# Re-ordering the first part of a Strassen gated-FFN kernel: scalings, normalisations and copies on ScalarE, the order of two token tiles, and the mask counts

## The chip, the cores and the metric

One core of one Trainium2 chip. The metric is device time of one execution in microseconds (us): median of three runs 524.1 (524.1, 522.62, 524.27). Engines are named as in the profile: PE is TensorE's matrix product, PEld its weight load, DVE VectorE, ACT ScalarE, POOL GpSimd, SP the engine that issues the DMAs. Each engine works through its instructions in order; an instruction that waits holds up all that stand behind it on its engine.

## What is computed

```python
def reference(data, weight, mask, ln_w, gate_w, up_w, down_w):
    x = data                                    # 2 x 1024 x 512, float32
    xn = _layernorm(x)                          # over the last axis
    block_mask = mask.reshape(nb, 32, kb, 32).astype(float32).sum(axis=(1, 3)) > 0
    w_masked = weight * (block_mask, each entry repeated over its 32 x 32 block)
    s = einsum('bsk,nk->bsn', xn, w_masked)     # 512 x 512 weight
    nx = xn * rsqrt(mean(xn^2) + 1e-5) * ln_w
    g = einsum('bsh,ih->bsi', nx, gate_w)       # 1792 x 512
    u = einsum('bsh,ih->bsi', nx, up_w)         # 1792 x 512
    f = einsum('bsi,hi->bsh', silu(g) * u, down_w)   # 512 x 1792
    return x + s * silu(f)
```

## The kernel before

**Tiling.** The 2048 tokens are four token tiles t = 0 to 3 of 512, each of four sub-tiles i of 128 rows; the 512 features are four chunks c of 128. A sub-tile is loaded (`load_x`, L119), its mean and variance are taken on DVE (`stats`, L125), a tile's scale and offset are made in three steps (`factors`, L130: DVE, a square root on ACT, DVE) and applied (`normalise`, L144, on ACT or DVE). PE turns it over chunk by chunk into a bank (`transpose`, L153), from which a copy (`evacuate`, L159, on ACT) or a subtraction (`outer_b`, L195, on DVE) reads it. `rms_factor` (L169) takes the RMS factor from the same variances: four small DVE operations and a square root on ACT.

**The products.** All products are made by a two-level Strassen scheme: seven outer products q, each of seven inner products m of 128x128 by 128x512. Weights come in seven groups g = 0 to 6 of gate and up rows, and the masked 512x512 weight as group 7. One pair (g, q) is an *instance* j (`instance`, L328): seven products into banks x (m = 1, 6, 7, 4), y (m = 5, 3) and z (m = 2). There are three banks X, two Y, one Z and two V; V holds transposes, gates and the small results. Within an instance: z is seeded with a copy of x on ACT before product 2 adds to it (L345); y and x are saved in the middle (a *snapshot*, L350 to L355, on ACT where there are no earlier sums to add, else an add on DVE); and the final values (*totals*, L357 to L365) are DVE adds, or an ACT copy where there is nothing to add. "x_2" below is bank x of instance 2.

Instances 0 to 15 are q = 1 and 2 of each group. They read only token tiles 0 and 1. Instances 16 to 55 are q = 6, 5, 7, 3, 4 of each group and need tiles 2 and 3 as well. After them, seven sets of 25 products with the down weights.

**Operands.** Token differences are made by `outer_b` (L195) and `inner_b` (L212), on DVE or POOL; weights are loaded (`load_a`, L255), scaled by ln_w in two halves (`scale_a`, L260, on ACT; group 7 is masked instead, `mask_a`, L284, on POOL), and summed on POOL: `inner_a` for q = 1, 2 (L307: four adds of 128x2x128), `outer_a` (L289: four adds of 128x512) for the other q, whose results are stored to DRAM (`store_w`, L300), loaded back later (`load_w`, L303) and summed by `inner_a` again (four adds of 128x5x128). The running sums of a group's first two instances are likewise stored (L454) and loaded back (L455, tensor `acc_dram`). The mask is loaded (`load_mask`, L270), summed along rows on DVE (`mask_rows`, L276), and summed over blocks by a product into a V bank, `pm` (`mask_blocks`, L279), after which DVE writes which blocks are kept.

**What sets the order.** The order is written by hand. `at(pos, fn)` (L69) puts a step at a position; at the end all steps are sorted by position (equal ones in the order in which they were put in) and emitted, and each engine's queue is that order restricted to its own instructions. Position 7*j + offset belongs to instance j: products stand at offsets 0, 2, 3, 4, 6, 8, 12 (m = 1, 5, 2, 6, 3, 7, 4), the snapshot or total one position after its product. One position is about 0.86 us, and `T(us) = (us - 14.9) / 0.86` (L641) turns a time into a position. Nothing but this order and the data decides when a step runs: what stands behind a waiting step on the same engine waits too.

The steps of the first part are in L664 to L751: statistics and normalisation of the tiles, transposes, evacuations, token differences (L682 to L718), scalings and weight sums per group (L721 to L742, with `p` the position of a group's instance q = 1, `rest` that of its q = 6), and the mask (L745 to L749).

Of the kernel before, what the change touches and what calls it, by code (L numbers as in the profile page):

```python
# [31 lines left out]
def tile_masked_linear_gated_ffn(  # L32
# [36 lines left out]
    def at(pos, fn, *args):  # L69
        events.append((pos, len(events), fn, args))  # L70
# [13 lines left out]
    def slot(tag, name=None):  # L84
        i, n = ring[tag]
        ring[tag][0] += 1
        return mem[:, first_slot[tag] + i % n, :]

    def slots(i, n):
        return mem[:, i : i + n, :]  # L90
# [3 lines left out]
    def bank(tag, name):  # L94
        return ps.tile([P, W], F32, tag=tag, name=name, bufs=PSB[tag])

    def add(eng, o, a, b, op=ALU.add):
        eng.tensor_tensor(o, a, b, op)  # L98

    dve, pool, act = nc.vector, nc.gpsimd, nc.scalar  # L100
# [68 lines left out]
    def rms_factor():  # L169

        def first():
            nc.vector.tensor_scalar_add(rms, agg[:, :, :, 1], EPS)
            nc.vector.reciprocal(rms, rms)
            nc.vector.tensor_mul(rms, agg[:, :, :, 1], rms)
            nc.vector.tensor_scalar_add(rms, rms, EPS)
        return [first, lambda: nc.scalar.activation(rms, rms, AF.Sqrt)]
# [72 lines left out]
    def w_slots(g):  # L249

        if g == 0:
            return F["q"], F["a1"] + 4
        return (F["s"], F["s"] + 5) if g % 2 else (F["q"], F["a1"] + 4)
# [53 lines left out]
    def inner_a(g, part, k0=0, n=2):  # L307

        if part == 1:
            i, si, qs = F["a1"] + 2 * (g % 3), F["s"] + 2 * (g % 2), (1, 2)  # L310
        else:
            i, si, qs = *w_slots(g), BLOCKS
        a, s = slots(i + k0, n), slots(si + k0, n)
        a11, a21, a12, a22 = (a[:, :, k * P : (k + 1) * P] for k in range(4))
        s1, s2, s3, s4 = (s[:, :, k * P : (k + 1) * P] for k in range(4))
        for k in range(n):
            aop[g, qs[k0 + k]] = {1: a11[:, k], 2: a12[:, k], 3: s4[:, k], 4: a22[:, k],
                                  5: s1[:, k], 6: s2[:, k], 7: s3[:, k]}
        return [lambda: add(pool, s1, a21, a22), lambda: add(pool, s2, s1, a11, ALU.subtract),
                lambda: add(pool, s4, a12, s2, ALU.subtract), lambda: add(pool, s3, a11, a21, ALU.subtract)]  # L320

    def weights(g, q, m):
        if q < 3 and m in (1, 2, 4):
            return aq[g, 0, q - 1][:, {1: 0, 2: 2, 4: 3}[m] * P :][:, :P]
        return aop[g, q][m]


    def instance(j, g, q, prior, dest, after):  # L328


        st = {}

        seeded = j > 0

        def mm(m, tag, key, first):
            if first and key not in st:
                st[key] = bank(tag, f"{key}_{j}")
            nc.tensor.matmul(st[key], weights(g, q, m), operand(q, m), start=first and not (key == "z" and seeded),  # L338
                             stop=True, skip_group_check=True)

        def seed():

            if seeded:
                st["z"] = bank("Z", f"z_{j}")
                nc.scalar.copy(st["z"], st["x"])  # L345
            else:
                st["s1"] = slot("s2", f"s1_{j}")
                nc.scalar.copy(st["s1"], st["x"])

        def snap(key, name, i):  # L350
            s = st[name] = slot(name, f"{name}_{j}")
            if prior is None:
                nc.scalar.copy(s, st[key])  # L353
            else:
                add(dve, s, st[key], prior(i))  # L355

        def total(key, name, i):  # L357
            if key == "z" and not seeded:
                name = "s1"
            if name:  # L360
                add(dve, dest(i), st[key], st[name])
            elif prior is None:
                nc.scalar.copy(dest(i), st[key])  # L363
            else:
                add(dve, dest(i), st[key], prior(i))  # L365

        at(EARLY.get((j, 0), 7 * j + 1), seed)
        for off, m, tag, first, snapshot, out in (
            (0, 1, "X", True, None, None),
            (2, 5, "Y", True, ("s5", 3), None),  # L370
            (3, 2, "Z", True, None, (None, 0)),
            (4, 6, "X", False, ("s2", 1), None),
            (6, 3, "Y", False, None, ("s2", 1)),
            (8, 7, "X", False, None, ("s5", 3)),
            (12, 4, "X", False, None, (None, 2)),
        ):
            key, pos = tag.lower(), 7 * j + off
            at(EARLY.get((j, m), pos), mm, m, tag, key, first)
            if snapshot:
                at(pos + 1, snap, key, *snapshot)  # L380
            elif out:
                at(pos + 1, total, key, *out)
                after(out[1], pos + 1)


    def group(g, where):
# [254 lines left out]
    T = lambda us: (us - 14.9) / 0.86  # L641
# [14 lines left out]
    def plan(pos, step, todo):  # L656
        for i, fn in enumerate(todo):
            at(pos + step * i, fn)
# [4 lines left out]
            nc.tensor.matmul(b[:, :P], ident, ident, start=True, stop=True, skip_group_check=True)  # L663

    at(T(1.4), lambda: warm(30, bank("V", "idle")))
    for t, p, step in ((0, T(8.2), 0), (1, T(13.4), 0), (2, 15.0, 1.3), (3, 22.0, 1.3)):
        plan(p, step, factors(t))
    for i in range(TT):
        half = act if i < 2 else dve
# [8 lines left out]
    at(T(8.2), scale_a, 0, 0, 1, pool)  # L678
    for c in range(KC):
        at(T((10.7, 11.3, 11.9, 14.0)[c]), evacuate, 0, c, act)  # L680
        at(T((17.4, 16.0, 18.9, 18.3)[c]), evacuate, 1, c, act)
    for us, q, m in ((15.9, 1, 5), (16.6, 1, 6), (17.2, 1, 7), (17.8, 2, 5), (18.4, 1, 4), (19.0, 2, 6),  # L682
                     (19.6, 2, 7), (20.3, 2, 4)):
        at(T(us), inner_b, q, m, dve)
# [2 lines left out]
            for n in (0, 1):  # L687
                at(8, outer_b, q, k, n, None)
    at(T(16.4), scale_a, 1, 0, 0)
    for i, (R, K, g) in enumerate(((0, 1, 1), (1, 0, 0), (1, 1, 0))):  # L690
        at(T(19.2 + 2 * i), scale_a, g, R, K)
    for i in range(TT):
        at(9.6 + 1.3 * i, stats, 2, i)
        at(17.2 + 1.3 * i, stats, 3, i)
        at(17.7 + 1.2 * i, normalise, 2, i, act)
        at(27.0 + 1.9 * i, normalise, 3, i, dve)
    plan(24.8, 1.3, rms_factor())

    for t, p0 in ((2, 31.0), (3, 45.0)):
        n = t % 2  # L700
        for k, c in enumerate((2, 3, 0, 1)):
            for i in range(TT):
                at(p0 + 2 * k + 0.01 * i, transpose, t, c, i, "V")
            if c >= 2:
                at(p0 + 2 * k + 1.2, evacuate, t, c, act)
            else:
                at(p0 + 2 * k + 1.2, outer_b, 5, c, n, dve)
                at(p0 + 2 * k + 1.21, outer_b, 7, c, n, dve)
    for k in (0, 1):
        for n in (0, 1):  # L710
            at(52, outer_b, 3, k, n, None)
    for n, p0 in ((0, 40), (1, 54)):
        for k in (0, 1):
            at(p0 + 1.5 * k, outer_b, 6, k, n, dve)
            at(p0 + 2.2 + 1.7 * k + (16 if n == 0 else 4), outer_b, 4, k, n, pool)
    for q, p in ((6, 57), (5, 66), (7, 76), (4, 89), (3, 113)):
        for off, m, eng in ((0, 5, dve), (3, 6, dve), (5.5, 7, pool), (7.5, 4, pool)):
            at(p + off, inner_b, q, m, eng)  # L718


    for g in range(G + 1):  # L721
        p, rest = 7 * where[g, 1], 7 * where[g, BLOCKS[0]]
        prepare = scale_a if g < G else lambda g, R, K: mask_a(R, K)
        for K in range(2):
            if g > 2:
                at(p - 22, load_a, g, 0, K)
            if g > 1:
                at(p - 14 + 1.5 * K, prepare, g, 0, K)
                at(p - 10, load_a, g, 1, K)
            if g > 0:  # L730
                at(p - 4 + 1.5 * K, prepare, g, 1, K)
        if g:
            plan(p - 8, 1, inner_a(g, 1))
        else:
            plan(T(7.4), 0, inner_a(0, 1, 0, 1))
            plan(T(10.0), 0, inner_a(0, 1, 1, 1))
        sums = {0: 10, G: p + 15}.get(g, p + 1)
        for i, q in enumerate((7, 5, 6, 3)):
            at(sums + 1.6 * i, outer_a, g, q, pool)
        at(sums + 7.5, store_w, g)  # L740
        at(rest - 29 if g else rest - 11, load_w, g)
        plan(rest - 13 if g else rest - 9, 2.5, inner_a(g, 2, 0, 5))  # L742
# [1 line left out]
        for off, fn in zip((8, 30, 32, 34, 36, 37), outer_d(f)):  # L744
            at(7 * where[f, BLOCKS[0]] + off, fn)  # L745
    for i, (R, K) in enumerate(QUADS):
        at(56, load_mask, R, K)
        at(63 + 2 * i, mask_rows, R, K)
    at(71, mask_blocks)  # L749
    at(120, rms_store)  # L750
    for t in range(NTT):  # L751
        at(END + 13, rms_rows, t)
# [17 lines left out]
    for o, q in enumerate(DOWN):  # L770
# [9 lines left out]
        for k, m in enumerate((5, 6, 7, 4)):  # L780
            pos = END + (-26, -17, -8, -5)[k] if o == 0 else D(o - 1)((3, 8, 12, 18)[k])
# [6 lines left out]
        for k in range(4):  # L788
            pos = END + (-22, -18, -11, -9)[k] if o == 0 else D(o - 1)(10) + 2.5 * k
# [84 lines left out]
```

## Time and profile before

| | |
|---|---|
| median of three runs | 524.1 us |
| profiled execution, its own time | 524.07 us |
| its span in the trace | 522.2 us (1.9 less) |
| granted TensorE clock | 1.00 |
| first product of instance 16 (first that needs tiles 2 and 3) | near 121.7 us |
| POOL busy | 378.2 us (72%) |
| ACT busy | 154.6 us (30%) |
| DMA queue 1 | 60000 packets, 137.53 MB, 73.8% of 16 engines' span |

Of the page's 40 slices (13 us each) these rows show the first part on the left:

```profile
PE   8889999999999999999999999999999999999996
DVE  5897798767696877959687896989645654457736
ACT  3868656431332232233233222321100101001111
POOL 5496689978896978969678896977544564739960
PEclk9999999999999999999999999999999999999999
DMA  9559798889829486575996867499897599476372
```

Each digit is the busy share of a slice in tenths, 9 being 90% or more. A line of a timeline reads: start, length, engine, line of the kernel, operation, output<-input, shape, number of instructions taken together, and in brackets the engine's idle time before it with what ended it. A line of a list of groups reads: line, engine, operation, shape, count | busy us, mean ns of one | idle before, with its main releaser. A line of the list of waits reads: engine, tile, line, what it waited for: us in all, times, the longest.

### The profile page before, as it was taken

How to read it: one execution, taken by the hardware profiler on the slowest of the kernel's cores; microseconds unless marked ns; L12 is line 12 of the kernel's file. 1: busy time of each engine (PE TensorE's matmuls, PEld its weight loads, DVE VectorE, ACT ScalarE, POOL GpSimd, SP SyncE). 2: the span in 40 equal slices, each digit the busy share in tenths (PEclk: the TensorE clock that was granted, in tenths of full speed). 3: DMA queues.
4: the chain of work that ended last, by engine and by line, in shares of the span. 5: the costliest groups of instructions: out<-in, count | busy, mean ns of one | idle time of the engine just before them, and what ended most of it. 6: DMA issues, size and time to landing. Idle time of an engine off the chain costs nothing.

```text
span 522.2 us, 4847 instructions
## 1 busy us (share of the span) xinstructions
PE 509.0 (97%) x1269; PEld 230.7 (44%) x1269; DVE 383.7 (73%) x557; ACT 154.6 (30%) x286; POOL 378.2 (72%) x301
## 2 busy tenths in 40 slices
PE   8889999999999999999999999999999999999996
PEld 8333443444444444444444444443444444444443
DVE  5897798767696877959687896989645654457736
ACT  3868656431332232233233222321100101001111
POOL 5496689978896978969678896977544564739960
PEclk9999999999999999999999999999999999999999
DMA  9559798889829486575996867499897599476372
GB/s 312 210 213 347 294 331 331 317 301 325 321 110 313 161 282 238 210 244 185 381 364 231 293 221 270 154 341 387 295 386 267 187 355 347 157 251 204 148 232 80
DMA packets 60314, 138.35 MB, mean 265 GB/s; under 512 B 5744, under 2 KB 13184, under 8 KB 56192
## 3 DMA queue, kind: packets, MB, share of 16 engines
q1 hardware_dynamic: 60000, 137.53, 73.8%
q10 hardware_dynamic: 288, 0.52, 0.3%
q8 instruction: 10, 0.16, 0.1%
q14 instruction: 16, 0.13, 0.1%
HBM read 81.40 MB, written 56.63 MB: 264 GB/s over the span
## 4 chain that ended last, share of the span: by engine, by line
PE 75%; DVE 9%; issue 2%; ACT 0%; DVEq 0%
PE x L338 26%; PE dx L557 14%; PE y L338 14%; PE dy L557 8%; DVE mem L98 7%; PE z L338 6%; PE dz L557 5%; DVE mem L402 2%; PE dv L557 1%; PE half L568 1%; DVE mask_sums L277 0%; DVE mem L547 0%; PE pm L281 0%; ACT silu L540 0%; DVEq L402 0%
## 5 line engine op out<-in xcount | busy, mean ns | idle before, releaser
L98 POOL TENSOR_TENSOR mem<-mem 128x512 f32<-128x512 f32 (+4 forms) x266 | 344.4, 1314 | 107.7 <-ACT mem L363 20.3
L338 PE MATMUL x<-mem 128*128 128x512 f32 x448 | 214.6, 595 | 4.0 <-ACT mem L353 2.4
L338 PEld LDWEIGHTS x<-mem 128*128 128x128 f32 x448 | 83.4, 190 | 109.2 <-issue 92.6
L98 DVE TENSOR_TENSOR mem<-x,mem 128x512 f32<-128x512 f32 x136 | 92.4, 685 | 45.6 <-PE x L338 44.3
L338 PE MATMUL y<-mem 128*128 128x512 f32 x224 | 114.8, 594 | 0.9 <-ACT mem L353 0.5
L98 DVE TENSOR_TENSOR mem<-mem 128x512 f32<-128x512 f32 (+2 forms) x93 | 106.9, 1151 | 7.6 <-PE dx L557 4.4
L557 PE MATMUL dx<-mem 128*128 128x512 f32 x174 | 78.3, 592 | 0.0
L98 DVE TENSOR_TENSOR mem<-y,mem 128x512 f32<-128x512 f32 x96 | 65.8, 685 | 15.5 <-PE y L338 12.8
L345 ACT COPY z<-x 128x512 f32<-128x512 f32 x55 | 31.4, 571 | 125.0 <-PE x L338 125.0
L338 PEld LDWEIGHTS y<-mem 128*128 128x128 f32 x224 | 41.8, 190 | 53.9 <-issue 47.3
L338 PE MATMUL z<-mem 128*128 128x512 f32 x112 | 57.4, 594 | 0.7 <-ACT z L345 0.7
L557 PEld LDWEIGHTS dx<-mem 128*128 128x128 f32 x174 | 33.1, 190 | 41.6 <-issue 40.7
L557 PE MATMUL dy<-mem 128*128 128x512 f32 x98 | 44.5, 592 | 0.0
L402 DVE TENSOR_TENSOR mem<-gate,mem 128x512 f32<-128x512 f32 x56 | 37.4, 681 | 1.7 <-ACT gate L397 1.2
L397 ACT ACTIVATE gate<-mem 128x512 f32<-128x512 f32 x56 | 33.1, 602 | 19.0 <-DVE mem L402 10.0
L530 POOL TENSOR_TENSOR mem<-mem 128x512 f32<-128x512 f32 x16 | 24.9, 1563 | 17.6 <-DMA mem<-s_dram 17.2
L338 PEld LDWEIGHTS z<-mem 128*128 128x128 f32 x112 | 20.9, 190 | 26.2 <-issue 22.3
L98 DVE TENSOR_TENSOR mem<-z,mem 128x512 f32<-128x512 f32 x41 | 28.0, 684 | 3.2 <-PE z L338 3.2
L557 PEld LDWEIGHTS dy<-mem 128*128 128x128 f32 x98 | 18.6, 190 | 23.4 <-issue 23.2
L540 ACT ACTIVATE silu<-mem 128x512 f32<-128x512 f32 x15 | 9.0, 602 | 64.6 <-DVE mem L98 48.3
L98 DVE TENSOR_TENSOR mem<-dx,mem 128x512 f32<-128x512 f32 x16 | 11.1, 691 | 20.1 <-PE dx L557 20.1
L557 PE MATMUL dz<-mem 128*128 128x512 f32 x56 | 25.2, 592 | 0.0
(61 smaller groups left out, 227.3 us busy)
## 6 DMA issues: line engine op xcount, KB each, us to landing
h_dram<-mem SPq DMA_DIRECT2D x98, 256.0 KB, 2.6
mem<-h_dram SPq DMA_DIRECT2D x28, 768.0 KB, 6.8
w_dram<-mem SPq DMA_DIRECT2D x8, 1280.0 KB, 6.2
mem<-w_dram SPq DMA_DIRECT2D x8, 1280.0 KB, 6.9
acc_dram<-mem SPq DMA_DIRECT2D x8, 1024.0 KB, 5.5
mem<-acc_dram SPq DMA_DIRECT2D x8, 1024.0 KB, 4.9
mem<-in_gu SPq DMA_DIRECT2D x28, 256.0 KB, 4.4
s_dram<-mem SPq DMA_DIRECT2D x16, 256.0 KB, 5.1
```

The costliest lines, as they stand in the source:

```text
L98: eng.tensor_tensor(o, a, b, op)
L338: nc.tensor.matmul(st[key], weights(g, q, m), operand(q, m), start=first and not (key == "z" and seeded), stop=True, skip_group_check=True)
L345: nc.scalar.copy(st["z"], st["x"])
L397: nc.scalar.activation(gate[key], t(), AF.Silu)
L402: nc.vector.tensor_mul(a(), gate[key], b())
L530: at_later.append(lambda: nc.gpsimd.tensor_tensor(s_tile, s_tile, rms_bc[t], ALU.mult))
L540: nc.scalar.activation(b[0][:, part], y[:, part] if source is None else source(), AF.Silu)
L557: nc.tensor.matmul(st[key], w(), b(), start=first and key != "z", stop=True, skip_group_check=True)
L568: nc.tensor.matmul(st[half.start][:, half], w(), b()[:, half], start=False, stop=True, skip_group_check=True)
```

## The change

Only positions change (and in one place the choice between two tiles' order); the instructions and DMAs are the same in kind and number.

- `total` on ACT (instances q = 1 and q = 5 that have nothing to add): the copy of z goes from one position behind its product to 2.3 behind it, which is after the snapshot of x.
- Tile 2: factors from position 15.0 to 14.5, statistics in steps of 1.2 instead of 1.3, normalisation on ACT at 30.2, 37.0, 40.9 and 44.0 instead of 17.7, 18.9, 20.1 and 21.3. Tile 3: normalisation on DVE at 26.5 + 2.4i instead of 27.0 + 1.9i. RMS factor from 24.8 to 22.2.
- Tile 1's evacuations of chunks 0, 2 and 3 from positions 2.9, 4.7 and 4.0 to 5.6, 6.0 and 3.14.
- Three early scalings (second half of group 1's first weights, group 0's second rows) from 5.0, 7.3 and 9.7 to 5.2, 8.7 and 9.8. In the queue of ACT their order against the evacuations and snapshots changes with that.
- Tile 3 is transposed at 37.5 and tile 2 at 51.5, where tile 2 stood at 31 and tile 3 at 45; the token differences that need them stand some six positions later, and for the two tiles in the other order.
- Per group: the scalings of the q = 1, 2 weights from p - 14 and p - 12.5 to p - 10.4 and p - 7.3; those of the other rows from p - 4 and p - 2.5 to p - 3.1 and p - 1.9 (group 2: p - 4.3 and p - 3.1); the inner weight sums start at p - 7 instead of p - 8.
- Mask: loads from 56 to 62, row sums from 63 in steps of 2 to 68 in steps of 1.5, block sums from 71 to 76.

```diff
--- before.py
+++ after.py
@@ -379,8 +379,10 @@
             if snapshot:
                 at(pos + 1, snap, key, *snapshot)
             elif out:
-                at(pos + 1, total, key, *out)
-                after(out[1], pos + 1)
+
+                pos += 2.3 if prior is None and m == 2 and seeded else 1
+                at(pos, total, key, *out)
+                after(out[1], pos)
 
 
     def group(g, where):
@@ -663,7 +665,7 @@
             nc.tensor.matmul(b[:, :P], ident, ident, start=True, stop=True, skip_group_check=True)
 
     at(T(1.4), lambda: warm(30, bank("V", "idle")))
-    for t, p, step in ((0, T(8.2), 0), (1, T(13.4), 0), (2, 15.0, 1.3), (3, 22.0, 1.3)):
+    for t, p, step in ((0, T(8.2), 0), (1, T(13.4), 0), (2, 14.5, 1.3), (3, 22.0, 1.3)):
         plan(p, step, factors(t))
     for i in range(TT):
         half = act if i < 2 else dve
@@ -678,7 +680,7 @@
     at(T(8.2), scale_a, 0, 0, 1, pool)
     for c in range(KC):
         at(T((10.7, 11.3, 11.9, 14.0)[c]), evacuate, 0, c, act)
-        at(T((17.4, 16.0, 18.9, 18.3)[c]), evacuate, 1, c, act)
+        at((5.6, T(16.0), 6.0, 3.14)[c], evacuate, 1, c, act)
     for us, q, m in ((15.9, 1, 5), (16.6, 1, 6), (17.2, 1, 7), (17.8, 2, 5), (18.4, 1, 4), (19.0, 2, 6),
                      (19.6, 2, 7), (20.3, 2, 4)):
         at(T(us), inner_b, q, m, dve)
@@ -687,16 +689,16 @@
             for n in (0, 1):
                 at(8, outer_b, q, k, n, None)
     at(T(16.4), scale_a, 1, 0, 0)
-    for i, (R, K, g) in enumerate(((0, 1, 1), (1, 0, 0), (1, 1, 0))):
-        at(T(19.2 + 2 * i), scale_a, g, R, K)
+    for pos, (R, K, g) in zip((5.2, 8.7, 9.8), ((0, 1, 1), (1, 0, 0), (1, 1, 0))):
+        at(pos, scale_a, g, R, K)
     for i in range(TT):
-        at(9.6 + 1.3 * i, stats, 2, i)
+        at(9.6 + 1.2 * i, stats, 2, i)
         at(17.2 + 1.3 * i, stats, 3, i)
-        at(17.7 + 1.2 * i, normalise, 2, i, act)
-        at(27.0 + 1.9 * i, normalise, 3, i, dve)
-    plan(24.8, 1.3, rms_factor())
-
-    for t, p0 in ((2, 31.0), (3, 45.0)):
+        at((30.2, 37.0, 40.9, 44.0)[i], normalise, 2, i, act)
+        at(26.5 + 2.4 * i, normalise, 3, i, dve)
+    plan(22.2, 1.3, rms_factor())
+
+    for t, p0 in ((3, 37.5), (2, 51.5)):
         n = t % 2
         for k, c in enumerate((2, 3, 0, 1)):
             for i in range(TT):
@@ -708,12 +710,12 @@
                 at(p0 + 2 * k + 1.21, outer_b, 7, c, n, dve)
     for k in (0, 1):
         for n in (0, 1):
-            at(52, outer_b, 3, k, n, None)
-    for n, p0 in ((0, 40), (1, 54)):
+            at(58, outer_b, 3, k, n, None)
+    for n, p0 in ((1, 46), (0, 60)):
         for k in (0, 1):
             at(p0 + 1.5 * k, outer_b, 6, k, n, dve)
-            at(p0 + 2.2 + 1.7 * k + (16 if n == 0 else 4), outer_b, 4, k, n, pool)
-    for q, p in ((6, 57), (5, 66), (7, 76), (4, 89), (3, 113)):
+            at(p0 + 2.2 + 1.7 * k + (16 if n == 1 else 4), outer_b, 4, k, n, pool)
+    for q, p in ((6, 63), (5, 70), (7, 78), (4, 90), (3, 113)):
         for off, m, eng in ((0, 5, dve), (3, 6, dve), (5.5, 7, pool), (7.5, 4, pool)):
             at(p + off, inner_b, q, m, eng)
 
@@ -725,12 +727,12 @@
             if g > 2:
                 at(p - 22, load_a, g, 0, K)
             if g > 1:
-                at(p - 14 + 1.5 * K, prepare, g, 0, K)
+                at(p - (10.4, 7.3)[K], prepare, g, 0, K)
                 at(p - 10, load_a, g, 1, K)
             if g > 0:
-                at(p - 4 + 1.5 * K, prepare, g, 1, K)
+                at(p - ((3.1, 1.9) if g != 2 else (4.3, 3.1))[K], prepare, g, 1, K)
         if g:
-            plan(p - 8, 1, inner_a(g, 1))
+            plan(p - 7, 1, inner_a(g, 1))
         else:
             plan(T(7.4), 0, inner_a(0, 1, 0, 1))
             plan(T(10.0), 0, inner_a(0, 1, 1, 1))
@@ -744,9 +746,9 @@
         for off, fn in zip((8, 30, 32, 34, 36, 37), outer_d(f)):
             at(7 * where[f, BLOCKS[0]] + off, fn)
     for i, (R, K) in enumerate(QUADS):
-        at(56, load_mask, R, K)
-        at(63 + 2 * i, mask_rows, R, K)
-    at(71, mask_blocks)
+        at(62, load_mask, R, K)
+        at(68 + 1.5 * i, mask_rows, R, K)
+    at(76, mask_blocks)
     at(120, rms_store)
     for t in range(NTT):
         at(END + 13, rms_rows, t)
```

## The prediction

> **What bounds the kernel now.** I read the page's first lines (busy time) and the kind of work in the chain that ended last, then the list of what PE waited for, then PE's timeline for where those waits are, and last the other engines' timelines around them.
>
> ```profile
> PE 509.0 (97%) x1269; PEld 230.7 (44%) x1269; DVE 383.7 (73%) x557; ACT 154.6 (30%) x286; POOL 378.2 (72%) x301
> PE 75%; DVE 9%; issue 2%; ACT 0%; DVEq 0%
> ```
> ```profile
> PE x L338 <- ACT mem L353: 2.4, 2, 1.3
> PE x L338 <- DVE mem L98: 1.5, 7, 0.2
> PE pm L281 <- DVE mask_sums L277: 1.2, 1, 1.2
> PE z L338 <- ACT z L345: 0.7, 1, 0.7
> ```
> ```profile
> 22.44 1.12 PE L338 MATMUL x<-mem 128*128 128x512 f32 x2 [1.13 <-ACT mem L353]
> 36.03 1.10 PE L338 MATMUL x<-mem 128*128 128x512 f32 x2 [1.31 <-ACT mem L353]
> 45.52 1.12 PE L338 MATMUL z<-mem 128*128 128x512 f32 x2 [0.66 <-ACT z L345]
> 85.77 0.41 PE L281 MATMUL pm<-mask_sums,blockones 128*128 128x64 f32 x2 [1.16 <-DVE mask_sums L277]
> ```
>
> PE is busy 509.0 of 522.2 us, and the granted clock is 1.00 throughout. Products start 0.858 us apart (74.70 to 76.42 is two). Adding up how far the starts fall behind that pitch from 17.5 us to 86 us gives 7.7 us. No reordering of this part can save more than that, and all the edits touch this part. The bulk of it: y_0 and x_0 waiting for ACT's snapshots (0.67 and 1.40; x_0 is bank x of instance 0), x_2's snapshot at 36.03 (1.47), transposes and z_4 at 44.5 to 48 (0.57, 0.88, 0.38), the mask counts (1.33).
>
> **Instances 0 and 1: the snapshots.** ACT's timeline of before:
>
> ```profile
> 19.06 0.59 ACT L164 COPY mem<-pt 128x512 f32<-128x512 f32 x1 [0.55 <-DVE mem L98]
> 19.54 0.59 ACT L353 COPY mem<-y 128x512 f32<-128x512 f32 x1
> 20.02 1.09 ACT L164 COPY mem<-pt 128x512 f32<-128x512 f32 x2
> 20.97 0.94 ACT L266 ACTIVATE mem<-mem,lnw_sb 128x256 f32<-128x256 f32 x2
> 21.78 0.60 ACT L353 COPY mem<-x 128x512 f32<-128x512 f32 x1
> ```
>
> The snapshot of y_0 stands behind an evacuation that waits 0.55 for DVE, and that of x_0 behind two more evacuations (1.09) and a scaling (0.94). In the new order y_0's snapshot comes directly after the scaling that ends at 18.6, x_0's after one evacuation: 18.64 + 0.59 = 19.23, one evacuation and its wait to 19.72, + 0.59 = 20.31. x_0's product 7 starts at 20.37 instead of 22.44, 2.07 earlier. Part of it goes at once. z_1's seed (ACT) now stands behind the evacuation of chunk 2, which must wait for the DVE add that still reads another chunk, and that ends at 22.02 in before; nothing ahead of it moves. 22.06 + 0.6 of evacuation + 0.5 to 0.6 of seed: z_1 at 23.2 instead of 24.26, 1.06 earlier. One more statistics pair comes ahead of x_1's snapshot on DVE: its product 7 goes from 28.55 to 28.06, so 0.49 is left there.
>
> **Tile 2's normalisation.** Four ACT operations at 33.42 (0.81 each) stood ahead of x_2's snapshot; they go to positions 30 to 44, behind it. x_2's product 7 then follows at pitch, 34.2 instead of 36.03: 1.8 earlier. The RMS factor's four DVE operations (0.78 together) now come ahead of x_2's total, so its product 4 starts at 38.17, not 39.66: 1.5 kept. Moving the copy of z behind the snapshot of x takes 0.5 from what a snapshot stands behind; in the instances that PE reaches at pitch it costs nothing, since only DVE's later adds read that copy.
>
> **The scalings and POOL's weight sums, to instance 4.** Group 1's second scaling runs at 20.2 instead of 20.97, so POOL starts those sums 0.8 earlier, the w store goes at 30.0 instead of 30.8, the load back is ready at 38.6 instead of 39.44. Behind that load on ACT stand, as in before:
>
> ```profile
> 39.44 1.70 ACT L266 ACTIVATE mem<-mem,lnw_sb 128x256 f32<-128x256 f32 x4 [1.52 <-DMA mem<-in_gu]
> 41.26 1.28 ACT L397 ACT_TABLE_LOAD   x1
> 42.55 1.12 ACT L397 ACTIVATE gate<-mem 128x512 f32<-128x512 f32 x2
> 44.89 0.58 ACT L345 COPY z<-x 128x512 f32<-128x512 f32 x1
> ```
>
> 38.62 + 1.70 + 1.28 + 1.12 with their gaps is 42.8, a copy of 0.5, the seed to 43.76: z_4 at 43.81 instead of 45.52, 1.7 earlier. With the third tile's transposes moved from position 31 to 51 (tile 3 comes first, at 37.5), the 0.57 at 44.5 has no counterpart there, and 0.38 at 48.05 and 0.16 at 58.21 go, less some 0.15 of a new wait at 45.85. I count from the second product into x_8, at 74.70 in before (call it T): T comes at 72.6, **2.1 earlier**.
>
> **POOL gives it back.** In before POOL has no gap from 67.02 on, after waiting 4.28 for a scaling:
>
> ```profile
> 67.02 31.79 POOL L98 TENSOR_TENSOR mem<-mem 128x512 f32<-128x512 f32 x26 [4.28 <-ACT mem L266]
> 98.76 1.05 POOL L287 TENSOR_TENSOR mem<-mem,keep 128x512 f32<-128x512 f32 x1
> 99.77 1.27 POOL L98 TENSOR_TENSOR mem<-mem 128x512 f32<-128x512 f32 x1
> ```
>
> Four of the adds from 68.25 on are outer differences of tokens (q=4), which in before run ahead of group 5's inner weight sums; those start at 78.78, T + 4.1. Now the differences stand six positions later, behind them, and group 5's scaling, 57.5 before, stands at 59.6 and 62.7. On ACT's queue it is behind x_8's snapshot, which waits for PE: T + 1.06, then snapshot 0.48, three copies and a scaling of 0.4 to 0.5 each, T + 3.4. POOL has nothing to do from about 71 (T - 1.5) to T + 3.5. From there the same 25 operations that took 78.78 to 107.44, 28.66 us, up to the first sum of group 7, plus the four differences, 4.92 at the undisturbed pitch of 1.23 (98.76 + 1.01 = 99.77, + 1.23 is the next entry's start) or 6.26 as they ran in before: **T + 37.1 to T + 38.4**. Against this, y_14, the first product that reads the sum, started at 110.96, T + 36.26, and the sum had ended at T + 32.74: 3.5 of slack, all used up.
>
> DVE's SBUF-only adds slow POOL's and decide between the two ends:
>
> ```profile
> L98 POOL TENSOR_TENSOR mem<-mem 128x512 f32<-128x512 f32 x22 | 30.6, 1409 | 4.6 <-ACT mem L266 4.3
> L98 DVE TENSOR_TENSOR mem<-mem 128x512 f32<-128x512 f32 x10 | 10.0, 1002 | 0.0
> ```
>
> A POOL add alone takes 1.27, one beside such a DVE add 1.72 (70.72, 72.39, 74.07), 0.45 more; the ten DVE adds of the window average 1.00 where one of a bank and a tile takes 0.68. I follow the 29 operations and meet eight overlaps: 18 x 1.23 + 9 x 0.70 + 2 x 1.01 + 0.6 for chained ones + 8 x 0.45 = 34.7, T + 38.1, near the upper end; I take that. y_14 then starts 1.85 later against T than before, and of the 2.1, **0.25 is left** (bounds: 0 to 1.25).
>
> The Trainium skill (SBUF — State Buffer, section "SBUF: two separate sides") says that the port pair of VectorE and GpSimd is an exclusive lock for a whole instruction, so that a VectorE operation with two SBUF inputs and a GpSimd one that reads SBUF don't share but block. By that rule each of the eight overlaps would cost up to the other's whole 0.68, 5.4 in place of 3.6, and the forecast would be some 1.8 higher. The trace has 0.45, less than the full block, and decides; but the rule speaks against packing more POOL work beside DVE's adds.
>
> **The mask counts.** The four mask loads go six positions later on SP's queue, past the stores and the weight loads of that stretch, one of which waits for a product near T + 1.9. They took 5.5 to 5.7 us (67.73 to 73.47, 70.53 to 76.06), so the first lands by T + 7.7, and its count stands at 68, T + 6.9: up to 0.8 of wait on DVE, which I cost at nothing since DVE had no gap from 76 to 86 (10.00 of 10.00 us busy) and so runs behind its order. The counts are 1.5 instead of 2 apart. The product pm at position 76 would come at pitch at T + 13.8, and waits for a DVE gate product that ends at T + 14.6 to T + 15.2: 0.8 to 1.4, where it was 1.33. This wait is moved, not removed; y_14's wait for POOL absorbs it.
>
> **What comes behind.** POOL's lateness delays group 6's w store, 106.78 to 108.9, and through it the load back (118.48 to 120.6 or later) and the sums that y_16 needs by 122.8. SP issues the load of group 0's running sums behind it, at 117.23, and DVE waited for that:
>
> ```profile
> 125.69 0.69 DVE L98 TENSOR_TENSOR mem<-y,mem 128x512 f32<-128x512 f32 x1 [1.16 <-DMA mem<-acc_dram]
> ```
>
> It landed at 125.60, 7.1 after the w load; y_16's second product follows that add, at 126.53. So whatever was gained before, y_16 comes no earlier than this load allows: the change of the time is the larger of -0.25 and the load's own lateness. That is bounded by 0 (it is issued by PE's pace, not POOL's) and 2.3 (7.1 behind a w load that lands 2.1 to 2.4 later, 127.9). The DMA share is 0.94 from 110 to 120 and 0.96 from 120 to 130: little room to catch up, 0.06 x 10 + 0.04 x 6 = 0.84. Of 2.1, 1.2 to 1.3 stay; I take 1.2. From position 112 on the two orders are the same but for the copies of z, so nothing further comes. **Sum: 524.07 (span 522.2 + 1.9 around it) + 1.2 = 525.3 us**. The profiled execution stands 0.03 below the median of the runs, so no correction is made.
>
> **Rivals.** What a measurement of this kernel can tell from no change is 0.3%, 1.57 us: 522.5 to 525.7.
> 1. *Even* (0.40): the above, 525.3; own range 523.8 (only the 0.25 counts) to 525.7.
> 2. *Faster* (0.26): POOL is no bound. If the four differences run undisturbed and two or three of the eight overlaps fall elsewhere, the sum is ready at T + 36.5, y_14 waits for nothing, the w store goes on time, and the load of the sums, whose issue goes with PE, comes two us earlier into DMA engines that were busy only 0.59 of 100 to 110: all 2.1 stay, 522.0. For it: DVE's adds are shifted by two us too, so the overlaps are not the same ones. Against it: in before they hit three of these four adds, and two things must go well.
> 3. *Slower* (0.34): the load of the sums queues behind the late w load as it did in before and keeps its 7.1: 524.07 + 2.3 = 526.4. The place is y_16, and it decides from 1.6 of lateness on. For it: shares of 0.94 and 0.96 leave next to no room. Against it: the load's issue at 117.23 is not late, and between 107 and 109 nothing but this store is held back.
>
> That the diff does not do what it says is small: tile 2's normalisation really leaves ACT's queue ahead of x_2's snapshot. The range of 521.9 to 526.6 reaches to both other cases, 0.1 to 0.2 beyond their prices.
>
> **What would show it.** Right: x_0's product 7 at 20.4, x_2's at 34.2, z_4 near 43.8, POOL idle some 5 us around 71 to 76, y_14's first product waiting for POOL near 110.7, and the load of the sums landing at 126.8, with y_16 waiting for it. Wrong: no POOL wait before y_14 (then faster), or a PE wait over 1 us between 24 and 72 that I have not listed, such as z_1's seed waiting longer.

## The result and the profile after

The changed kernel takes 523.81 us (median of four runs, 523.43 to 524.09) against 524.18 us before (four runs, 522.62 to 524.84): a ratio of 0.9997 with a 95% interval of 0.9974 to 1.0020. No difference can be told. The profiled execution after has a span of 521.6 us, 0.6 less than before's 522.2.

The page's busy times and the kind of work in the chain that ended last, of the changed kernel:

```profile
PE 508.3 (97%) x1269; PEld 230.2 (44%) x1269; DVE 384.6 (74%) x557; ACT 153.4 (29%) x286; POOL 376.1 (72%) x301
PE 73%; DVE 11%; DMA 7%; POOL 4%; issue 3%; ACT 1%; SPq 0%; DVEq 0%; POOLq 0%
```

In before that chain was PE and DVE; now it passes through POOL (4%) and DMA (7%). PE's list of waits names the place:

```profile
PE x L338 <- DVE mem L98: 2.4, 9, 0.4
PE y L338 <- POOL mem L98: 1.9, 1, 1.9
...
PE y L338 <- DVE mem L98: 1.2, 1, 1.2
PE z L338 <- ACT z L345: 0.8, 2, 0.5
...
PE pm L281 <- DVE mem L404: 0.6, 1, 0.6
PE x L338 <- DMA mem<-w_dram: 0.3, 1, 0.3
```

The two long waits for ACT's snapshots (2.4 us in before) are gone. In their place stand one wait of 1.9 for POOL, one of 1.2 for DVE and one of 0.3 for the w load. Where they are (PE's timeline after; line numbers are two higher than before's from L382 on):

```profile
108.73 1.12 PE L338 MATMUL y<-mem 128*128 128x512 f32 x2 [1.86 <-POOL mem L98]
119.61 1.98 PE L338 MATMUL x<-mem 128*128 128x512 f32 x4 [0.32 <-DMA mem<-w_dram]
364.37 1.13 PE L338 MATMUL y<-mem 128*128 128x512 f32 x2 [1.16 <-DVE mem L98]
```

Following the same products in both traces gives the account of the gain. T, x_8's second product, falls from 74.70 to 70.95: 3.75 us. Just ahead of y_14 (109.24 in before, 104.98 after) the lead is 4.26. At y_14 it is 2.23 (110.96 against 108.73), at x_16 1.65 (121.26, a little before the 121.7 of the table above, against 119.61), and it stays at 1.5 to 1.6 up to 361 us. After y_55, near 364, it is 0.65, and that is what reaches the end. So an early gain of about 4 us was given back in three places: 2.0 at y_14, 0.6 at x_16, 0.9 at y_55. Some 0.5 of the early gain is scatter: already the first product of y_0 stands at 17.06 instead of 17.57, and over the kernels below that have this part unchanged it stands anywhere from 17.06 to 17.79. So most of the 0.65 between the two profiles may be that scatter.

POOL around T, after (ACT first, then POOL):

```profile
72.01 0.59 ACT L353 COPY mem<-x 128x512 f32<-128x512 f32 x1 [0.33 <-PE x L338]
72.50 0.59 ACT L363 COPY mem<-z 128x512 f32<-128x512 f32 x1
72.97 0.62 ACT L399 ACTIVATE gate<-mem 128x512 f32<-128x512 f32 x1
73.50 0.90 ACT L266 ACTIVATE mem<-mem,lnw_sb 128x256 f32<-128x256 f32 x2
```
```profile
64.44 5.34 POOL L98 TENSOR_TENSOR mem<-mem 128x512 f32<-128x512 f32 x4 [0.70 <-ACT mem L266]
74.48 3.90 POOL L98 TENSOR_TENSOR mem<-mem 128x256 f32<-128x256 f32 x4 [4.71 <-ACT mem L266]
```

x_8's snapshot stands at 72.01, T + 1.06, and waits for PE; behind it come two ACT operations and only then the second half of group 5's scaling, which ends at 74.40. POOL waits 4.71 us for it and restarts at 74.48, T + 3.53. It then works without a gap to speak of, and group 7's first sum ends at 108.67, T + 37.72. y_14 starts 0.06 later.

### The profile page after: what moved, and what is told of

It is laid out like the page before. It is cut to its first block, busy times and chain, and to the rows that moved or that the text cites. A ratio compares the mean times of both kernels' runs of the same rounds, so it can differ in the third digit from the quotient of the medians.

```text
span 521.6 us, 4847 instructions
## 1 busy us (share of the span) xinstructions
PE 508.3 (97%) x1269; PEld 230.2 (44%) x1269; DVE 384.6 (74%) x557; ACT 153.4 (29%) x286; POOL 376.1 (72%) x301
## 4 chain that ended last, share of the span: by engine, by line
PE 73%; DVE 11%; DMA 7%; POOL 4%; issue 3%; ACT 1%; SPq 0%; DVEq 0%; POOLq 0%
PE x L338 24%; PE dx L559 14%; PE y L338 13%; PE dy L559 8%; DVE mem L98 7%; PE z L338 6%; PE dz L559 5%; POOL mem L98 3%; DMA w_dram<-mem 2%; DVE mem L404 2%; DMA mem<-w_dram 2%; DMA mem<-h_dram 1%; PE dv L559 1%; DMA mem<-in_mask 1%; PE pt L156 1%
## 5 line engine op out<-in xcount | busy, mean ns | idle before, releaser
L98 DVE TENSOR_TENSOR mem<-mem 128x512 f32<-128x512 f32 (+2 forms) x93 | 108.6, 1171 | 8.2 <-PE dx L559 4.4
L559 PEld LDWEIGHTS dx<-mem 128*128 128x128 f32 x174 | 33.1, 190 | 41.6 <-issue 40.9
L532 POOL TENSOR_TENSOR mem<-mem 128x512 f32<-128x512 f32 x16 | 24.4, 1526 | 17.7 <-DMA mem<-s_dram 17.4
```

Source lines behind the costliest of these rows:

```text
L532: at_later.append(lambda: nc.gpsimd.tensor_tensor(s_tile, s_tile, rms_bc[t], ALU.mult))
L559: nc.tensor.matmul(st[key], w(), b(), start=first and key != "z", stop=True, skip_group_check=True)
```

## The experiments

Each ran beside the kernel before on the same chip; the ratio is to that. e1 to e4 and e9 to e12 ran on one chip, e5 to e8 on another, so for a comparison across these rows both the medians and the ratios are given.

| kernel | median us (lowest to highest) | before | ratio, 95% interval |
|---|---|---|---|
| changed kernel | 523.81 (523.43 to 524.09) | 524.18 | 0.9997, 0.9974 to 1.0020 |
| e1 all groups' scalings and sums back | 523.01 (521.70 to 525.87) | 523.93 | 0.9988, 0.9972 to 1.0004 |
| e2 two token differences early | 521.58 (521.09 to 522.39) | 523.93 | 0.9955, 0.9940 to 0.9970 |
| e3 tile 2's normalisation back | 524.40 (523.11 to 525.16) | 523.93 | 1.0007, 0.9996 to 1.0018 |
| e4 before, early ScalarE part alone | 524.51 (523.53 to 526.31) | 523.93 | 1.0008, 0.9994 to 1.0021 |
| e5 only group 5 back | 520.99 (520.61 to 521.13) | 523.88 | 0.9953, 0.9936 to 0.9969 |
| e6 e2 and the tail edit | 520.19 (519.72 to 520.79) | 523.88 | 0.9940, 0.9925 to 0.9955 |
| e7 changed kernel and the tail edit | 523.21 (522.37 to 523.87) | 523.88 | 0.9990, 0.9978 to 1.0001 |
| e8 changed kernel, early ScalarE part undone | 523.33 (522.32 to 524.84) | 523.88 | 0.9993, 0.9980 to 1.0007 |
| e9 e5 and the tail edit | **519.94** (519.59 to 520.02) | 524.02 | **0.9918**, 0.9904 to 0.9933 |
| e10 e5, e2 and the tail edit | 520.62 (519.32 to 522.47) | 524.02 | 0.9936, 0.9913 to 0.9959 |
| e11 e9 with the early ScalarE part undone | 520.17 (519.86 to 520.98) | 524.02 | 0.9929, 0.9912 to 0.9945 |
| e12 before and the tail edit | 523.64 (522.81 to 524.92) | 524.02 | 0.9992, 0.9982 to 1.0001 |

**e1: the group scalings and sums back.**

```diff
-                at(p - (10.4, 7.3)[K], prepare, g, 0, K)
+                at(p - 14 + 1.5 * K, prepare, g, 0, K)
-            plan(p - 7, 1, inner_a(g, 1))
+            plan(p - 8, 1, inner_a(g, 1))
```

> The changed kernel with one part undone: each group's q = 1, 2 scalings at p - 14 and p - 12.5 and its inner weight sums from p - 8, as before the change. Theory (POOL's idle stretch near 70 to 74 us, caused by group 5's scaling standing behind x_8's snapshot on ACT, is what makes y_14 wait 2.0 us): the idle stretch of about 5 us is gone, the first sum of group 7 ends 4 us or more earlier, y_14 does not wait, and 1.5 to 2 us of it reach the end: 521.8 to 522.3. Rival (something behind y_14, the w load, the load of the running sums or the end of the groups, sets the end anyway): y_14's wait goes but reappears between 115 and 130 us or at the tail, 523.3 to 524.

y_14's wait is gone: group 7's first sum ends at 106.70, 2 us earlier, and y_14 comes at 108.62 without waiting. But the end gains less than the theory said (523.01), because an early wait came back:

```profile
42.37 0.90 ACT L266 ACTIVATE mem<-mem,lnw_sb 128x256 f32<-128x256 f32 x2
43.18 0.58 ACT L345 COPY z<-x 128x512 f32<-128x512 f32 x1
```
```profile
43.81 1.12 PE L338 MATMUL z<-mem 128*128 128x512 f32 x2 [1.68 <-ACT z L345]
```

In ACT's and PE's timelines of e1, a scaling of 0.9 stands again between the gates and z_4's seed, and z_4 waits 1.68. By its position it is group 3's: the place p - 14 is position 28, ahead of the seed at 29, where the change has it at 31.6. So this edit moved two things of opposite sign, group 5's steps and group 3's. Neither the theory nor the rival of this run had it.

**e5: group 5 alone back**, the other groups as changed.

```diff
-                at(p - (10.4, 7.3)[K], prepare, g, 0, K)
+                at(p - ((14, 12.5) if g == 5 else (10.4, 7.3))[K], prepare, g, 0, K)
-            plan(p - 7, 1, inner_a(g, 1))
+            plan(p - (8 if g == 5 else 7), 1, inner_a(g, 1))
```

> The changed kernel with the q = 1, 2 scalings and inner weight sums of group 5 alone back at p - 14, p - 12.5 and p - 8 (the other groups stay as changed). Theory (group 5's late scaling makes POOL idle near 70 us; in the run with all groups put back, the wait of 1.8 us at z_4 came from group 2's scalings, not from group 5's): POOL's idle stretch goes, no wait at y_14, and z_4 waits less than 1.1 us; end 521.6 to 522.4, as for the two token differences moved early. Rival (all groups' places count, or the idle stretch has another cause): y_14 still waits over 1 us or z_4 1.8, end 522.8 to 524.

It is 520.99, even below what was expected, and z_4 waits for nothing (the wait of e1 was group 3's, though, and not group 2's as this expectation has it). Group 5's two scalings now stand at 66.71 and 68.86 on ACT, ahead of x_8's snapshot at 72.25. POOL's timeline of e5 shows one stretch where the changed kernel had a gap, and the windows of the two kernels (us; PE, PEld, DVE, ACT and POOL busy, granted clock, DMA share, GB/s) show the same for 62 to 82 us, the changed kernel's two lines first:

```profile
64.68 13.41 POOL L98 TENSOR_TENSOR mem<-mem 128x512 f32<-128x512 f32 x11 [0.69 <-ACT mem L266]
```
```profile
62.00:72.00 10.00, 10.00 (x37) 5.26 (x36) 7.32 (x12) 5.89 (x12) 6.76 (x7) 1.00 0.69 282
72.00:82.00 10.00, 9.89 (x23) 4.10 (x23) 9.38 (x15) 5.74 (x12) 7.44 (x8) 1.00 0.91 285
```
```profile
62.00:72.00 10.00, 10.00 (x36) 5.17 (x35) 7.33 (x12) 6.60 (x14) 8.84 (x10) 1.00 0.71 290
72.00:82.00 10.00, 9.79 (x23) 4.01 (x22) 10.00 (x14) 4.92 (x10) 10.00 (x8) 1.00 0.94 321
```

POOL's busy time in these 20 us rises from 14.2 to 18.8. T is at 71.19 there; the first sum ends at 105.48, T + 34.3 instead of T + 37.7, and y_14 starts at T + 36.26 (107.45) without a wait, exactly where before had it against its T. x_16 does not wait either. This shows the cause: the later places of one group's two scalings, four instructions on ACT, and of the sums behind them cost the changed kernel 2.3 us by the ratios, 2.8 by the medians. The waits at y_14 and x_16 make up 2.2 of it.

**e2: POOL's gap filled instead.** The two differences of tile 3 go where POOL is idle.

```diff
-            at(p0 + 2.2 + 1.7 * k + (16 if n == 1 else 4), outer_b, 4, k, n, pool)
+            at(p0 + 2.2 + 1.7 * k + (8 if n == 1 else 4), outer_b, 4, k, n, pool)
```

> The changed kernel with only two POOL adds moved: the q = 4 token differences of tile 3 (n = 1) from positions 64.2 and 65.9 to 56.2 and 57.9, where POOL is idle. Theory: two adds of 1.23 us fit into POOL's idle stretch, the first sum of group 7 ends 2.5 us earlier, y_14's wait falls from 2.0 to below 0.5, and the end comes 1.2 to 2 us earlier, 521.8 to 522.6. Rival (overlaps with DVE's adds and not the count of adds set POOL's end): the sum comes less than 1.3 us earlier and the end moves by less than 0.8, 523.0 to 523.8.

521.58: as the theory said. The first sum ends at T + 35.4 (107.08, T 71.65), 2.3 us earlier against T, where 2.5 was expected; POOL's wait of 4.71 is down to 3.11, and y_14 does not wait. Two different edits that have only POOL's lateness in common cure the same wait.

**e3 and e4: parts of the early change.** e3 takes tile 2's normalisation back to positions 17.7 to 21.3; e4 gives the kernel before only tile 1's evacuations, the three scalings and the copy of z.

> The changed kernel with tile 2's normalisation back at positions 17.7 to 21.3 on ACT, ahead of x_2's snapshot. Theory (POOL restarts a fixed 3.5 us after x_8's second product, so what is lost early arrives at y_14): x_2's product 7 waits 1.3 to 1.8 us again, x_8 and y_14 come 1.2 to 1.8 later, end 524.8 to 525.6. Rival (y_14's wait of 2.0 has room for it): the end stays at 523.6 to 524.0.

> The kernel before with one part of the change alone: tile 1's evacuations, the three early scalings and the copy of z behind the snapshot of x. Theory: x_0's product 7 comes 2 us earlier and z_1 about 1, but x_2's snapshot still stands behind tile 2's normalisation, which waits for DVE's factors near 33.4 us, so x_2's product 7 takes most of it back: 0 to 0.6 us earlier at 40 us, end 523.5 to 524.2. Rival (the gain at z_1 of about 1 us is kept): end 522.8 to 523.2.

e3 came out between theory and rival, 524.40. The place was not the one expected: x_2's product 7 does not wait, since its snapshot has only two normalisations ahead of it, not waiting for factors; the other two stand ahead of the next seed, and the next z (36.90) waits 0.59 of idle time. POOL's restart moves with T, as the theory has it (75.52, T + 3.52), and y_14 comes 1.0 later (109.77, again after 1.85 of waiting), x_16 waits 0.79. But 0.7 of that is a later start of this profiled execution (y_0's first product at 17.79 instead of 17.06); counted from there, T is 0.3 later.

e4 ends no earlier than before (524.51, where 523.5 to 524.2 was expected), but not for the reason given. x_2's product 7 still waits 1.02 for its snapshot at 34.68, as the theory has it. Yet it comes 1.35 earlier than in before, z_4 comes 1.03 earlier (44.49 against 45.52), and a lead of 0.96 is left at the product of y ahead of y_55's wait (360.14 against 361.10): up to there the rival's gain of about 1 us is kept. It goes at y_55, which waits 1.15 in e4 and 0.32 in before:

```profile
364.89 1.12 PE L338 MATMUL y<-mem 128*128 128x512 f32 x2 [1.15 <-DVE mem L98]
```
```profile
365.02 1.12 PE L338 MATMUL y<-mem 128*128 128x512 f32 x2 [0.32 <-DVE mem L98]
```

So e4 does not show the early ScalarE part to be worth nothing: in its profile the end of the groups hides it.

**e8 and e11: the early ScalarE part undone**, on the changed kernel and on e9.

```diff
-                pos += 2.3 if prior is None and m == 2 and seeded else 1
+                pos += 1
...
-        at((5.6, T(16.0), 6.0, 3.14)[c], evacuate, 1, c, act)
+        at(T((17.4, 16.0, 18.9, 18.3)[c]), evacuate, 1, c, act)
...
-    for pos, (R, K, g) in zip((5.2, 8.7, 9.8), ((0, 1, 1), (1, 0, 0), (1, 1, 0))):
-        at(pos, scale_a, g, R, K)
+    for i, (R, K, g) in enumerate(((0, 1, 1), (1, 0, 0), (1, 1, 0))):
+        at(T(19.2 + 2 * i), scale_a, g, R, K)
```

> The changed kernel without its earliest ScalarE part: tile 1's evacuations, the three early scalings and the copy of z as they stood before. Theory (the first 2 us of gain at x_0 are taken back to about 1 at z_1, and the later parts keep theirs): x_0 waits 1.3 to 2 again, T and y_14 come 0.5 to 1.2 later than in the changed kernel, end 524.3 to 525. Rival (waits further on, at x_1 and z_4, absorb it): 523.6 to 524.0.

> As the kernel with group 5 back and the tail edit, but with tile 1's evacuations, the three early scalings and the copy of z as before the change. The same undoing on the changed kernel did not make it slower by its median (523.33 against 523.81), with y_14 0.7 later and no wait at y_55. Theory (the early ScalarE part is worth 0.5 to 1.0 us, which the tail's wait of 0.9 hid): 0.4 to 1.0 slower than with it. Rival (waits at z_1 and x_1 take all of it): within 0.3.

By the medians the theory fell in both. e8 is 523.33, no slower than the changed kernel: in its profile y_14 comes 0.7 later, but x_16 does not wait and y_55 waits 0.32 instead of 1.16. e11 is 520.17 against e9's 519.94, 0.2 apart with runs that overlap (0.6 apart by the ratios). In e11 y_0 waits 0.51 and x_0 1.13, as in before, and z_1 and x_1 wait for nothing; in e9 these two start 0.7 and 0.6 behind the pitch. The profiles show more than the medians: counted from y_0's first product (17.10 in e11, 17.63 in e9) T comes at 54.57 in e11 and at 53.75 in e9, and the 0.8 are still there at y_14. On the clock, e11's earlier start hides most of it. So the two waits at y_0 and x_0, which look like 2 us in before's profile, leave 0.8 at T, and the runs can't tell what of that reaches the end from nothing.

**e6, e7, e9, e12: the tail edit.** The DVE subtraction for the first down set that stands ahead of y_55's snapshot is put ten positions later.

```diff
-            pos = END + (-26, -17, -8, -5)[k] if o == 0 else D(o - 1)((3, 8, 12, 18)[k])
+            pos = END + (-26, -17, -8, 2)[k] if o == 0 else D(o - 1)((3, 8, 12, 18)[k])
```

> The kernel with the two token differences early (521.58 before this) and, at the end of the groups, one DVE subtraction of 128x1536 (the last one for the first down set, needed only some 15 us later) moved from ahead of y_55's snapshot to ten positions later. Theory (that subtraction is blocked by a POOL add that began 0.3 us before it and holds y_55's snapshot up, so PE waits 1.2 us near 363): the wait goes, end 520.3 to 520.8. Rival (the next DVE or POOL operation takes its place, or the down set then waits for the subtraction): 521.3 to 521.9.

> The changed kernel with that one DVE subtraction moved and nothing else. Theory: 1.0 to 1.3 us less than the changed kernel, 522.5 to 522.9, with y_14's wait of 2.0 as in the changed kernel. Rival: 523.6 to 524.0.

> The changed kernel with group 5's scalings and inner weight sums back (520.99 before this) and the last subtraction of the first down set later. Theory (two separate losses, POOL at y_14 and the blocked subtraction at y_55): the second goes too, 0.7 to 1.3 less, 519.7 to 520.3. Rival (without it the next wait takes over): 520.7 to 521.1.

> The kernel before with only the subtraction of the first down set moved. Theory (in the profile of before the subtraction was not blocked and y_55 waited 0.3): 0 to 0.5 less, 523.4 to 523.9. Rival (before has the blocked subtraction in most executions, so the change did not cause the tail's loss): 0.8 to 1.3 less, 522.6 to 523.1.

In the profiles y_55 waits 1.1 to 1.2 in the changed kernel and in e1 to e5, 0.3 in before and e8, and not at all where the subtraction is moved. From e5 to e9 the edit brings 1.05 us by the medians (all runs of the one below all of the other) and 1.8 by the ratios, from e2 to e6 1.4 and 0.8; e6 ends just below what was expected. e12 gains 0.4, within what its theory said, with an interval that just holds 1: this suggests that in before the wait is short in most executions. e7 is inconclusive: 523.21, half of what was expected, and its interval can't be told from the changed kernel's. In its profile y_55's wait is gone, but y_14 waits 1.82 and x_16 now 0.71 instead of 0.32. That POOL's lateness takes part of it there is what the trace suggests; no run separates it.

**e10: both cures and the tail edit.**

> As the kernel with group 5 back and the tail edit, and the two token differences early as well. Theory (both edits cure the same wait at y_14, so they do not add): within 0.4 of the kernel without the differences. Rival (POOL still sets the pace behind y_14, through the w store and its load back): another 0.8 to 1.5 less.

520.62, with runs from 519.3 to 522.5. It is no faster than e9, and no run reached the 518.4 to 519.1 of the rival, so the rival is refuted: once y_14 does not wait, these two adds bring nothing more. That it would be slower can't be told; its profile has waits of 0.78 at z_4 (42.82) and 0.42 at 81.74.

## Why the prediction was right where it was, and wrong where it was not

The forecast was 525.3 and "even"; 523.81 lies in the range, and "even" is what was measured. The mechanism that decided was the one named: POOL, idle behind group 5's late scaling, gives the early gain back at y_14. The sum came 1.5 us too high, and three errors in it partly cancel. By the profiles, the lead at y_14 was 2.23 instead of 0.25. The load of the running sums was to take 1.45 from there on, and 0.6 went, at x_16. And 0.9 went at y_55, for which nothing was counted. Together that is -2.0, -0.9 and +0.9, the 1.9 us by which the profiled execution (523.43) lies below the sum. So that the time is so near to "even" is partly luck: without the loss at y_55 that execution would have taken about 522.5, the edge of what the prediction calls even. The range, 521.9 to 526.6, held both rivals' prices.

- **POOL gives it back: right.** Forecast: idle from T - 1.5 to T + 3.5, first sum of group 7 at T + 38.1 (37.1 to 38.4), y_14 waiting for it. Measured: idle from 69.8, T - 1.2, to T + 3.53; T + 37.72; a wait of 1.86; y_14 starts at T + 37.78, 1.5 later against T than in before, where 1.85 was forecast. e2 and e5 remove it in two ways.
- **T 2.1 earlier: mis-sized.** It is 3.75. About 0.5 of that is scatter of the start. 0.9 is z_4: it was forecast at 43.81, 1.3 behind the pitch, and came at 42.45, 0.4 behind it with a wait of 0.26. The step that failed is the load ready at 38.6 (the row's wait is for `in_gu`, a load of weight rows that SP issues behind the w store, not for the load back of the prediction's text):

```profile
36.57 0.89 ACT L266 ACTIVATE mem<-mem,lnw_sb 128x256 f32<-128x256 f32 x2
38.05 0.91 ACT L266 ACTIVATE mem<-mem,lnw_sb 128x256 f32<-128x256 f32 x2 [0.59 <-DMA mem<-in_gu]
38.98 1.28 ACT L399 ACT_TABLE_LOAD   x1
...
41.80 0.59 ACT L345 COPY z<-x 128x512 f32<-128x512 f32 x1
```

  I carried over before's transfer times. The store of the sums ahead of it took 3.8 us (26.32 to 30.1) instead of 5.9, and the w store 4.5 instead of 5.8, so the first of the loads was there at 36.4. The first scaling then ran before the second load landed, and the gates and the seed follow 1.4 us earlier than forecast.
- **x_0, z_1, x_1: right place by place.** Counted from y_0's first product, x_0's product 7 comes 2.07 earlier (at 19.86), as forecast, z_1 1.09 (at 22.66; forecast 1.06) and x_1's product 7 0.41 (at 27.63; forecast 0.49). z_1 waits for its seed and x_1 for DVE, also as forecast. How much of it reaches the end stays open (e4, e8, e11).
- **Tile 2's normalisation: right in kind, with one row misread.** The wait of 1.31 at 36.03 is gone. But of the four operations only two stood ahead of x_2's snapshot in before; the other two follow it:

```profile
33.42 0.81 ACT L149 ACTIVATE mem<-mem,nb,scl 128x512 f32<-128x512 f32 x1 [1.83 <-DVE nb L139]
34.14 0.56 ACT L363 COPY mem<-z 128x512 f32<-128x512 f32 x1
34.60 0.81 ACT L149 ACTIVATE mem<-mem,nb,scl 128x512 f32<-128x512 f32 x1
35.32 0.57 ACT L353 COPY mem<-x 128x512 f32<-128x512 f32 x1
35.78 1.52 ACT L149 ACTIVATE mem<-mem,nb,scl 128x512 f32<-128x512 f32 x2
```

  ACT's wait of 1.83 for DVE's factors is the larger part of what held the snapshot up, and tile 2's statistics and factors stand earlier in the change as well. Putting the normalisation back (e3) costs 0.5 to 0.6, less than the 1.5 counted, and the intervals can't tell that from nothing.
- **pm: right in kind.** It waits for DVE's gate product, as forecast, and comes 0.74 behind pitch, just under the 0.8 to 1.4 forecast, instead of 1.33.
- **The load of the running sums, +1.2: this term failed, and it carried the whole plus of the forecast.** The load's issue in SP's timeline before, then SP's and DVE's timelines after:

```profile
117.23 0.38 SPq L455 DMA_DIRECT2D mem<-acc_dram  x1
```
```profile
106.89 0.33 SPq L301 DMA_DIRECT2D w_dram<-mem  x1
...
111.39 0.32 SPq L305 DMA_DIRECT2D mem<-w_dram  x1
...
115.11 0.60 SPq L457 DMA_DIRECT2D mem<-acc_dram  x1
```
```profile
123.40 0.69 DVE L98 TENSOR_TENSOR mem<-y,mem 128x512 f32<-128x512 f32 x1 [1.01 <-PE z L338]
```

  POOL's w store was issued at 106.89, not 108.9: T was earlier than forecast, so the lateness against T was none on the clock. The load of the sums went out 2.1 us earlier with PE, at 115.11, and landed at 123.3, 3.7 us after the w load, not 7.1. From its issue to its landing it took 8.2 us, against 8.4 in before: in both traces the landing goes by the issue, not by the w load ahead of it. The DMA share from 110 to 130 rose to 1.00, so the room that I saw as missing was partly a load waiting for its issue. DVE's add then waits for PE. The rival "slower", which needed those 7.1, did not come; the rival "faster" did not either, since y_14 waited.
- **"From position 112 on the two orders are the same, so nothing further comes": wrong by 0.9.** The order is the same, the phase is not. y_55's product 3 waited 0.32 in before and 1.16 in after. The lines of DVE and POOL there, before and then after:

```profile
359.75 1.75 DVE L98 TENSOR_TENSOR mem<-mem 128x1536 f32<-128x1536 f32 x1
362.62 1.74 DVE L98 TENSOR_TENSOR mem<-mem 128x1536 f32<-128x1536 f32 x1
359.91 2.72 POOL L98 TENSOR_TENSOR mem<-mem 128x512 f32<-128x512 f32 x1
```
```profile
361.13 2.58 DVE L98 TENSOR_TENSOR mem<-mem 128x1536 f32<-128x1536 f32 x1
360.83 1.27 POOL L98 TENSOR_TENSOR mem<-mem 128x512 f32<-128x512 f32 x1
```

  In before the POOL add began 0.16 after a DVE subtraction (359.75) and took 2.72 instead of 1.27: POOL paid. In after POOL's began 0.30 ahead of DVE's, and DVE paid: 2.58 instead of 1.74, and y_55's snapshot stands behind it. It is not simply how early the kernel is: e8, ahead of before by 1.3 us there, has the short wait (0.32), and e3, level with before at 361 us, the long one.

## What to carry to other kernels

A step that waits for PE sets the time of all that stands behind it on its engine; when work for a third engine is put behind such a step, count what that engine will lose while idle and how much slack its consumer has, here 3.5 us of slack against 5 us of idling. A wait that the profile shows early is worth only what the next waits leave of it: two delays of 2 us in all at y_0 and x_0 left 0.8 some fifty products later, and what of that reached the end could not be told from nothing. Count such gains from a fixed product and not from the clock, since the start alone moved by up to 0.7. And undo a change in parts that are as small as the mechanism: taking back all groups at once (e1) hid most of a gain of over 2 us that one group alone (e5) showed.

## What was not expected of the hardware

In the pairs looked at here, an operation of DVE and one of POOL that both work on SBUF alone did not slow each other in proportion: the times fit if the one that starts second stands still until the first has all but ended. The pairs near 360 us show it with long operations (+1.45 for POOL beside a DVE subtraction of 1.75 that had begun 0.16 before; +0.84 for DVE beside a POOL add that had 0.97 to go). The prediction read 0.45 from short overlaps as "less than the full block". In before's trace that 0.45 is the rest of a DVE add which had itself waited for POOL's (DVE 70.27 to 71.30, the next POOL add from 70.72 to 72.43). The Trainium skill's rule in SBUF — State Buffer, section "SBUF: two separate sides", that the port pair is locked for a whole instruction, agrees with these rows. In these two traces it was a few tenths of a us of phase that decided who pays, and so edits before 90 us changed a wait at 364 by 0.8.
